# The order of VectorE, ScalarE and GpSimd in a decoder layer, taken from the scheduler with its simulated timeline switched on

## The chip, the cores and the metric

The kernel runs on one core of one Trainium2 chip. A core has five engines that each work through a queue of their own: TensorE (PE in the profile: matmuls and transposes; its loads of stationary operands are shown as PEld), VectorE (DVE), ScalarE (ACT), GpSimd (POOL) and SyncE (SP, which here only issues transfers). The metric is the device time of one execution in microseconds, as the median of several runs. Besides, one execution of each kernel is profiled; its time and its span (from the first to the last instruction) are given with it.

## The reference

It is one decoder layer in float32, with a batch of 32 sequences of 100 tokens, 256 wide:

```python
x = x + attn(layernorm(x))                    # 16 heads of 16, rotary positions, causal
x = x + xattn(layernorm(x), ctx, ctx)         # 16 heads, 361 context rows a sequence
x = x + soft_moe(layernorm(x))                # 8 experts of 128 slots each, 1024 hidden
```

The first attention has four projections (Wq, Wk, Wv, Wo) and a rotation of the queries and keys. The second has the same projections with biases, and its keys and values come from `ctx`. The third step is a soft mixture of experts: the normalised tokens are scored against 8 x 128 slot embeddings, a softmax over the tokens forms each slot, every slot goes through its expert's two layers with an exact GELU between them, and a softmax over the slots brings the results back to the tokens.

## The kernel before

**Tiles and stages.** The sequences are worked on in eight groups of four. For each group and each of the eight experts, `run_expert` multiplies the slots of four sequences (512 columns) by the first weight matrix in eight chunks (`ph`, line 893), applies GELU on ScalarE (`hT`, line 899), and multiplies by the second (`pe`, line 910). `route` (line 839) prepares an expert's slots (`dT`, `cT`, `disp`, `slT`), and `combine` (line 920) adds its result to the tokens (`py`, `x`).

**Six streams.** While the experts of one group run, the attention work of the next is fitted between the matmuls. It is written as Python generators: `self_attention` (line 487), `cross_softmax` (678), `crossing` (756), `cross_queries` (656), `cross_context` (669) and `prepare` (773, logits for the routing). Each yields a time before which its next step is not wanted. The function `between` inside the main loop (line 983) is called after every matmul of an expert and advances the streams whose time has come, by a count of TensorE time that the kernel keeps itself (`pe["t"]`). This fixes the order in which instructions are recorded.

**What fixes the order in the queues.** The kernel is built with the Tile layer. It takes the recorded instructions, works out who depends on whom, gives out the buffers of each pool in turn and places the semaphores. Every matmul and transpose is recorded through these two helpers, which pin it behind whatever was recorded on TensorE before it:

```python
def matmul(out, lhsT, rhs, share=1, **kw):                                    # line 87
    tc.keep_in_program_order(nc.tensor.matmul(out, lhsT=lhsT, rhs=rhs, **kw))
def transpose(out, in_, identity):                                            # line 91
    tc.keep_in_program_order(nc.tensor.transpose(out, in_, identity))
```

Instructions of the other engines are not pinned. Where several of them could go next on an engine, Tile's scheduler chooses when the program is built, and it may choose another order than the recorded one. On the chip, nothing is chosen any more.

**The steps that the change and the prediction touch.** In the first attention, `layer_norm` (line 315) makes `xh` on VectorE and GpSimd: statistics (306, 308), then `ve`, `rstd` and `xh` on GpSimd (310, 312, 318). TensorE transposes it, ScalarE copies `xhT` out of the bank (330), TensorE projects `ps_qk`, VectorE and GpSimd rotate (`ropeu`, `ropet`: 392 to 395), and ScalarE writes the rotated keys:

```python
nc.scalar.activation(                                                         # line 398
    kT[:, :, r, :], by(t)[:, 1], AF.Copy, scale=half[:, r : r + 1]            # rotk, read by the next sc
)
```

After the score matmuls `sc` come the mask (430), a maximum (436), a subtraction on GpSimd (437), the exponential on ScalarE (441), a sum (442) and its inverse `wide` (344). `self_turn` transposes the probabilities in four parts (`ps_pT`), and ScalarE copies each (`pT`, line 460). In the second attention, `context` transposes the context (`ps_cT`; copied as `ctxT`, 552) and projects the keys (`ps_kT`; copied with a bias as `kT`, 564); scores `xsc` are reduced (`xnmax`, 612) and exponentiated (`xp`, 617), turned (`xpT`, 633 and 635) and multiplied. `tokens` (742) makes the normalised tokens `xn` for the experts on GpSimd (310, 312, then 747 to 752), which TensorE transposes again.

At the start, `load_constants` (205) issues the loads of all attention weights and of the slot embeddings `se` from ScalarE's queue, `slots` (259) squares these on ScalarE (264) and scales them on VectorE (269) before TensorE turns them (`ps_sn`). SyncE issues the loads of `x` (292), of the context (534, 538) and of the experts' weights and biases (721 to 725). Each load counts on one of eight semaphores in turn, and a load waits at its issue until the one before it on the same semaphore has landed.

TensorE results go to banks of PSUM, 128 x 512 each: four for the scores, and two pools of two (`mm` and `big`) that `bank` (95) hands out. A bank is written again only after the copy out of it is done. ScalarE needs one table of functions for the exponential and another for GELU, so a change between them shows as an ACT_TABLE_LOAD.

## Time and profile before

| what | value |
|---|---|
| median of 3 runs | 3285.83 us (3285.1 to 3289.5) |
| profiled execution, its own time | 3288.43 us |
| its span | 3286.7 us |
| TensorE matmuls busy | 3087.9 us, 94% |
| VectorE, ScalarE, GpSimd busy | 1271.9, 1464.3, 547.1 us |
| mean granted TensorE clock | 0.979 |
| costliest groups: `pe` (L88), `ph` (L88) | 1047.6 us in 4096 matmuls, 1003.8 us in 2048 |
| ACT_TABLE_LOAD at the GELU line (L899) | 147, mean 1283 ns |

The page names an instruction by its line, its engine, and its output and inputs, with buffer numbers left out. The list of waits gives, for each engine, which result it was idle for: the total in us, how often, and the longest one. The order of time gives start, duration, engine, line and operation of merged instructions, and in brackets the idle time of the engine before them with the work that ended it. A float32 matmul shows as two passes, a transpose as one.

### The profile page before, as it was taken

To read this page: it belongs to the slowest core of one execution; us is meant where nothing else is said; L and a number is where in the kernel's file an instruction comes from. 1 tells how busy PE (TensorE), PEld (TensorE's weight loads), DVE (VectorE), ACT (ScalarE), POOL (GpSimd) and SP (SyncE) were. 2 spreads that over 40 slices of the span, in tenths; PEclk is the share of its full clock that TensorE was granted. 3 is DMA by queue.
4 is the path that set the end of the run, shared out by engine and by line. 5 is a ranking of instruction groups with operands and counts; after the bars stand their busy time and mean duration, and the time that the engine had idled before them with its cause. 6 is when DMAs were issued, how large, how long until landed. Compare 5 with 4: busy or idle time off the path is not lost.

```text
span 3286.7 us, 45298 instructions
## 1 busy us (share of the span) xinstructions
PE 3087.9 (94%) x18737; PEld 2158.8 (66%) x18737; DVE 1271.9 (39%) x2477; ACT 1464.3 (45%) x2846; POOL 547.1 (17%) x720
## 2 busy tenths in 40 slices
PE   5779999999999999999899999999899999999999
PEld 4656666665667666776666766667666766667666
DVE  3554443343433344334343344433443433332211
ACT  2444444444544544444454544544354444434331
POOL 3321321032111221012110121102311111100000
PEclk9789999999999999999999999999999999999999
DMA  3001111111111211212111111112111121112121
GB/s 107 5 10 32 45 43 57 48 42 47 55 50 42 69 45 42 64 43 67 43 45 51 61 49 47 55 50 63 41 54 47 45 64 55 42 59 68 61 64 57
DMA packets 116318, 167.55 MB, mean 51 GB/s; under 512 B 4520, under 2 KB 99728, under 8 KB 116112
## 3 DMA queue, kind: packets, MB, share of 16 engines
q1 hardware_dynamic: 112368, 161.01, 15.4%
q10 hardware_dynamic: 3744, 3.65, 0.4%
q8 instruction: 147, 2.41, 0.3%
q14 instruction: 59, 0.48, 0.0%
HBM read 161.36 MB, written 3.28 MB: 50 GB/s over the span
## 4 chain that ended last, share of the span: by engine, by line
PE 78%; ACT 10%; DVE 5%; POOL 4%; issue 2%; DMA 0%; ACTq 0%; DVEq 0%; POOLq 0%
PE pe L88 24%; PE ph L88 22%; PE sl L88 3%; PE ps_xpT L92 3%; PE py L88 3%; ACT xp L617 3%; PE xsc L88 3%; PE ps_xv L88 2%; PE ps_xav L88 2%; ACT L899 2%; PE ps_lt L88 2%; DVE xnmax L612 2%; PE ps_o L88 2%; PE ps_qk L88 2%; ACT hT L899 2%
## 5 line engine op out<-in xcount | busy, mean ns | idle before, releaser
L88 PE MATMUL pe<-w,hT 128*128 128x256 f32 x4096 | 1047.6, 388 | 15.3 <-ACT hT L899 14.9
L88 PE MATMUL ph<-slT,w 128*128 128x512 f32 x2048 | 1003.8, 604 | 29.1 <-ACT hT L899 28.8
L88 PEld LDWEIGHTS pe<-w,hT 128*128 128x128 f32 x4096 | 738.8, 192 | 169.6 <-issue 62.9
L899 ACT ACTIVATE hT<-ph,cols 128x512 f32<-128x512 f32 x512 | 350.0, 688 | 531.0 <-PE ph L88 508.6
L88 PEld LDWEIGHTS ph<-slT,w 128*128 128x128 f32 x2048 | 356.9, 191 | 294.3 <-issue 213.4
L617 ACT ACTIVATE xp<-xsc,xnmax 100x361 f32<-100x361 f32 x512 | 280.9, 563 | 116.5 <-DVE xnmax L612 80.6
L612 DVE TENSOR_REDUCE xnmax<-xsc 100x2 f32<-100x722 f32 x256 | 220.8, 899 | 166.2 <-PE xsc L88 165.4
L92 PEld LDWEIGHTS ps_xpT<-ident,xp 100*128 100x128 f32 (+1 forms) x1536 | 175.6, 153 | 114.2 <-issue 75.5
L635 DVE COPY xpT<-ps_xpT 128x400 f32<-128x400 f32 (+1 forms) x256 | 144.0, 570 | 211.3 <-PE ps_xpT L92 210.6
L899 ACT ACT_TABLE_LOAD x147 | 188.6, 1283 | 78.5 <-PE ph L88 76.2
L916 DVE TENSOR_TENSOR eo<-pe,b 128x512 f32<-128x512 f32 x128 | 87.9, 687 | 338.7 <-PE pe L88 338.3
L92 PE MATMUL ps_xpT<-ident,xp 100*128 100x100 f32 (+1 forms) x1536 | 192.0, 254 | 9.2 <-ACT xpT L633 5.8
L929 DVE SCALAR_TENSOR_TENSOR x<-py,cinv,x 100x256 f32<-100x256 f32 x256 | 112.2, 479 | 193.1 <-PE py L88 193.1
L856 POOL TENSOR_TENSOR dT<-dT,ri 128x400 f32<-128x400 f32 x64 | 54.4, 852 | 765.2 <-DVE ri L855 666.0
L437 POOL TENSOR_TENSOR p<-p,nmax 100x800 f32<-100x800 f32 x64 | 96.1, 1522 | 384.1 <-DVE nmax L436 382.2
L310 POOL TENSOR_SCALAR ve<-bnmv 100x1 f32<-100x1 f32 x96 | 21.4, 225 | 799.4 <-DVE bnmv L308 797.6
L88 PEld LDWEIGHTS sl<-disp,xn 100*128 100x128 f32 x1024 | 134.5, 194 | 14.9 <-DVE x L929 4.2
L849 POOL TENSOR_TENSOR cT<-lt,nmB 128x400 f32<-128x400 f32 x64 | 66.0, 1038 | 466.1 <-PE py L88 319.2
L88 PE MATMUL sl<-disp,xn 100*128 100x128 f32 x1024 | 137.4, 278 | 4.5 <-DVE x L929 2.7
L88 PE MATMUL xsc<-kT,xqT 32*100 32x361 f32 x1024 | 112.7, 510 | 22.8 <-ACT xp L617 21.0
L88 PE MATMUL py<-eo,cT 128*100 128x256 f32 x512 | 132.4, 381 | 1.0 <-DVE eo L916 0.8
L874 DVE TENSOR_SCALAR slT<-sl,cols 128x512 f32<-128x512 f32 x128 | 95.8, 749 | 72.5 <-PE sl L88 72.3
(140 smaller groups left out, 3457.4 us busy)
## 6 DMA issues: line engine op xcount, KB each, us to landing
w<-in_L_ffn_w_dram SPq DMA_DIRECT2D x128, 1024.0 KB
ctx<-in_ctx_dram SPq DMA_DIRECT2D x32, 256.0 KB
b<-in_L_ffn_b_dram SPq DMA_DIRECT2D x64, 128.0 KB
ctx<-in_ctx_dram SPq DMA_DIRECT2D x32, 105.0 KB
x<-in_x_dram SPq DMA_DIRECT2D x8, 400.0 KB
out_dram<-x SPq DMA_DIRECT2D x16, 200.0 KB
se<-n_L_ffn_slot_embeds_dram ACTq DMA_DIRECT2D x1, 1024.0 KB
rawWk<-in_L_attn_Wk_dram ACTq DMA_DIRECT2D x1, 256.0 KB
```

Of the source, the lines that this page charges most:

```text
L88: tc.keep_in_program_order(nc.tensor.matmul(out, lhsT=lhsT, rhs=rhs, **kw))
L92: tc.keep_in_program_order(nc.tensor.transpose(out, in_, identity))
L437: nc.gpsimd.tensor_tensor(p[:, hs, :], p[:, hs, :], nmax[:, hs].unsqueeze(2).to_broadcast([S, HPC, S]), ALU.subtract,)
L612: nc.vector.tensor_reduce(nmax[:, c, q : q + 2, r], sc[:S, q : q + 2, :SK], axis=AX.X, op=ALU.max, negate=True,)
L617: nc.scalar.activation(p[:, q, :], sc[:S, q, :SK], AF.Exp, bias=nmax[:, c, q, r : r + 1], accum_out=sums[:, c, q, r : r + 1],)
L635: nc.vector.tensor_copy(pT[:n], ps[:n, : HG * S])
L849: nc.gpsimd.tensor_tensor(cT, k.lt[e], k.nmB, ALU.add)
L856: nc.gpsimd.tensor_tensor(dT, dT, ri.unsqueeze(2).to_broadcast([P, nb, S]), ALU.mult)
L874: nc.vector.tensor_scalar(slT[:, dc, :], sl[:, : nb * NS], cols[:, NGM + dc : NGM + dc + 1], None, ALU.mult)
L899: nc.scalar.activation(h[:, :n], ph_[:, :n], AF.Gelu, bias=cols[:, e * NHC + hc : e * NHC + hc + 1])
L916: nc.vector.tensor_tensor(eo[:, :m], po[:, :m], b2.unsqueeze(1).to_broadcast([P, m, D]), ALU.add)
L929: nc.vector.scalar_tensor_tensor(xg[g][:, b, :], py[:S, i, :], k.ci[:, b : b + 1], xg[g][:, b, :], ALU.mult, ALU.add,)
```

## The change

The scheduler of the Tile layer is told to run a simulated timeline while it puts the instructions in order. Which instruction of an engine counts as ready, when the scheduler looks for the next one, then comes from that timeline. The instructions, their tiles and the order in which they are recorded stay as they are.

```diff
-    with _tile.TileContext(nc) as tc:
+    with _tile.TileContext(nc, schedule_with_timeline_sim=True) as tc:
         decoder_layer(tc, aps, *outs)
```

In the built program TensorE's instructions stand in the same order as before. Those of VectorE, ScalarE and GpSimd stand in a partly different one, four transfers of SyncE change places near the start, and table loads fall where ScalarE's new order needs them. The semaphores follow from the order.

## The prediction

> **What bounds the kernel now.** I read the busy table, then the waits of TensorE alone, then the order of time around the longest of them.
>
> ```profile
> span 3286.7 us, 45298 instructions
> ...
> PE 3087.9 (94%) x18737; PEld 2158.8 (66%) x18737; DVE 1271.9 (39%) x2477; ACT 1464.3 (45%) x2846; POOL 547.1 (17%) x720
> ```
>
> TensorE is the bound: 94% of the span, the others 45% at most. All that another order of VectorE, ScalarE and GpSimd can win is the remaining 199 us of TensorE idle time, 78 of it before 280 us (the windows of 20 us sum to 202.4 busy of 280), some 20 of those before any input is there. The rest is about 3 to 5 us in each 100. In the waits of TensorE (total us, times, longest) the top lines are these.
>
> ```profile
> PE ps_qk L88 <- ACT xhT L330: 34.0, 5, 22.9
> PE ph L88 <- ACT hT L899: 28.8, 28, 1.7
> PE ps_pT L92 <- ACT kT L564: 22.0, 4, 7.2
> PE xsc L88 <- ACT xp L617: 21.0, 17, 3.0
> PE pe L88 <- ACT hT L899: 14.9, 12, 2.2
> ```
>
> The third matters most: four waits, 22.0 us, so three of them are 7.2 us long. The order of time finds them at 779.07, 1568.99 and 2360.56 us, once every two groups. The first, on TensorE, then on ScalarE, then on GpSimd:
>
> ```profile
> 771.25 0.62 PE L88 MATMUL pe<-w,hT 128*128 128x256 f32 x2
> 779.07 0.91 PE L92 MATMUL ps_pT<-ident,p 100*100 100x100 f32 x4 [7.20 <-ACT kT L564]
> ```
> ```profile
> 777.75 0.81 ACT L398 ACTIVATE rotk<-ropet,half 128x200 f32<-128x200 f32 x2 [10.38 <-POOL ropet L395]
> 778.47 0.54 ACT L564 ACTIVATE kT<-ps_kT,cols 128x361 f32<-128x361 f32 x1
> 778.92 0.48 ACT L460 COPY pT<-ps_pT 100x400 f32<-100x400 f32 x1
> ```
> ```profile
> 774.39 1.24 POOL L318 TENSOR_SCALAR xh<-x,bnmv,rstd 100x256 f32<-100x256 f32 x1
> 775.59 1.02 POOL L394 TENSOR_TENSOR ropeu<-ropeu,rope 128x400 f32<-128x400 f32 x1
> 776.70 1.02 POOL L395 TENSOR_TENSOR ropet<-ropet,ropeu 128x400 f32<-128x400 f32 x1
> ```
>
> The matmuls of ps_kT had ended by 770.6. The copy out of their bank (kT, L564) stood behind rotk (L398), which waited 10.38 us for GpSimd, which worked off a string of layer-norm steps first. TensorE needed the bank.
>
> [...] The trace has 1283 ns as the mean of a load[...] (the load at 1216.06 us is followed by a GELU at 1217.35), so I charge 1.28 us. [...] I therefore take TensorE from starts: at 783.66 to 784.12 us the same pair of pe passes took 0.46 us from start to next start, so of 779.07 - 771.25 = 7.82 us some 7.4 is lost, against 7.20 shown; I use 7.2.
>
> **The change, part by part.** No operation is added or removed but table loads. From the built programs: all 10921 matmuls stand in the same order (each is pinned); of the other instructions 511 of 2445 on VectorE, 301 of 2014 on ScalarE (table loads apart), 305 of 720 on GpSimd and 4 of some 280 transfers on SyncE change place, by at most 11. So the question is where the first TensorE reader of each moved result stands. I went through the three queues and SyncE's in the new order: each instruction keeps its own duration from the trace, starts when the one ahead is through and its inputs are there, and hands on with the delays that the trace shows (34 to 95 ns); matmuls keep their start-to-start distances. The same treatment of the old order finds the old waits; I use differences alone.
>
> Rotk and kT. The new order at 779 us (and alike at the other two) is kT, four pT copies (L460), then rotk. kT then starts when ps_kT is done, the bank is free at about 771.3, and 7.2 us of idle go, three times: -21.6 us. The added wait: rotk stands behind the third and fourth pT copies, which wait for TensorE, so it comes about 1.7 us after its input. Behind it waits a copy of xnT (L330) that is not due yet. Its reader is the matmul group sc at 814.10 us, over 30 us on: it costs nothing.
>
> GELU before exponentials. At 1218 us TensorE waits for hT:
>
> ```profile
> 1215.17 0.87 ACT L441 ACTIVATE p<-p 100x800 f32<-100x800 f32 x1 [0.61 <-POOL p L437]
> 1216.06 1.28 ACT L899 ACT_TABLE_LOAD   x1
> 1217.35 1.27 ACT L899 ACTIVATE hT<-ph,cols 128x512 f32<-128x512 f32 x2
> ```
>
> The new order puts that first hT ahead of both exponentials of p. Waits of 0.9 (445 us), 2.2 (1218) and 2.2 (2010) go: -5.3 us. In all there are 302 table loads instead of 294; 8 x 1.28 = 10.3 us on an engine that is 45% busy. Were ScalarE late at every one of them, +10.3 would be the upper end; most replace idle time, and where they make a copy late it is in the rest below.
>
> The start. Now eight squares (L264) that wait for slot embeddings until 30.68 us keep the xhT copy back to 33.89, and TensorE waits 22.9 us. In the new order xhT comes before them. But ScalarE issues the embeddings' load later: its issue waits for the transfer of x (L292) that landed at about 26 us and that now has another place among the load semaphores, so the copies of ctxT and xhT end at about 28.9 and TensorE goes on 5.3 us earlier. The embeddings land 10.5 us after their issue (20.15 to 30.66 before), about 36.8; the squares (8 x 0.39), their scaling (L269, 8 x 0.27) and so ps_sn come 3.6 us late. With the later small gains and losses up to 280 us: -1.3 us. Bounds: -6 if the embeddings land as early as before, +5 if x lands 5 us later. Moving the ctx loads ahead of x on SyncE by two places is in this; nobody needs that ctx before 49 us.
>
> Late xn. GpSimd now takes the layer-norm chains of several sequences step by step side by side, with xn (L752) last. At 663 us two xh (1.23 each), an addition (0.81) and one ve and rstd (0.23 + 0.56) go ahead of it: 4.1 us, and its reader waited 0.33 us already, so none is covered. 22 of 32 xn come 0.8 to 7.7 us later, but most have room: +4.2 at 663, +1.2 at 2747, +0.4 at 1451 and 2243, together +6.2 us.
>
> The rest, some fifty places of both signs (+3.4 at 398 and +2.6 at 450 for xhT behind four exponentials; -2.8 at 349 and -2.7 at 549 for copies set free; +0.9 twice where wide, L344, is later and a wait of 4.6 us grows), adds to -3.8 us by the same working. It hangs on single tenths, so I count half: -2.
>
> Sum: -21.6 - 5.3 - 1.3 + 6.2 - 2 = **-24 us**. The profiled execution took 3288.4 us, 1.7 more than its span, and gives 3264.4; the median of the runs is 2.6 lower, so I predict **3262 us**. An early stall taken from TensorE stays won, as its later order is fixed[...].
>
> **Rivals.** *Given back.* The three waits go, but the start costs +5 and the rest is +5 instead of -2: -21.6 - 5.3 + 5 + 6.2 + 5 = -11, 3275 us. For it: most late copies sit in the first 700 us, where TensorE's idle share is largest; against: that stretch nets -1.1 by my working. *The wait moves.* If the pT copy rather than kT gates TensorE, or GpSimd is late to another reader at the same places, only the small gains stay: -2 to -6, 3282 us. Against: the pT copy now before 779 had its input at 771.4, and takes 0.48 us. A change without effect is excluded by the number of moved instructions. *Slower: GpSimd's chains.* Place: xn at the 32 ends of a sequence. Six are already late (9 us if TensorE were not shifted, 6.2 as counted); the next have room of 1.1, 3.6, 3.6 and five times 4.8 us. Were each xn d us later than its durations say, the cost is 6d + (d-1.1) + 2(d-3.6) + 5(d-4.8): at d = 4.8 it is 35 us, over the 24 won by more than 6.6. So it decides from about 4.8 us on, more than a third of a burst of 9 to 13 us; GpSimd's steps are steady in the trace. It gives 3294 us or more.
>
> **How the numbers follow.** Forecast 0.73, given back 0.15, wait moves 0.07, slower 0.05. 0.2% (6.6 us) is about what a measurement of this kernel can tell from no change. The first two are faster by more than that, so faster 0.88, within 0.07, slower 0.05. Handing on with doubled delays in both orders turns the sum to -31, and the early landing adds -5, so the low end is -38, 3248; the high end is the given-back case with a little more, 3277.
>
> **What would show it.** Right: no 7.2 us wait of ps_pT on kT; pe on hT with nothing above 1.5; ps_qk's longest about 17 to 18 us; ps_sn waiting for se some 3.6 us near 40 us; ps_xhT on POOL xn with a wait of about 4 near 660; 302 table loads; TensorE's busy time as before, and its idle time near 175. Wrong: the pT transposes at about 772, 1555 and 2340 us waiting on another engine for several us, or xn waits in every group.

## The result and the profile after

The changed kernel took 3266.09 us (median of 4 runs, 3265.5 to 3266.6) against 3285.47 us before (4 runs, 3283.9 to 3289.5): a ratio of 0.9939, 95% interval 0.9922 to 0.9956, 19.4 us less. The forecast was 3262 us, 24 us less than the median before. The total is near; several of the terms behind it, as the runs below show, are not.

The page of the changed kernel, the span and the busy table:

```profile
span 3264.1 us, 45284 instructions
...
PE 3079.0 (94%) x18737; PEld 2154.7 (66%) x18737; DVE 1273.4 (39%) x2477; ACT 1478.3 (45%) x2854; POOL 544.1 (17%) x720
```

TensorE's matmuls are the same 18737 passes (the 4096 and 2048 in the table before count passes as well), and yet their busy time fell by 8.9 us (3087.9 before). Its idle time fell by 13.7 us, from 198.8 to 185.1. I had forecast some 24 us of idle time and nothing in the busy time. ScalarE has eight instructions more, the eight table loads. All 302 take 1283 ns, and 301 of them stand where a GELU follows an exponential or an exponential a GELU (293 of 294 before); the other is ScalarE's first, at L552.

TensorE's waits in the changed kernel (result waited for, total us, times, longest):

```profile
PE ps_qk L88 <- ACT xhT L330: 32.7, 10, 13.7
PE ph L88 <- ACT hT L899: 26.5, 25, 1.7
PE xsc L88 <- ACT xp L617: 21.4, 20, 3.0
PE ps_xhT L92 <- POOL xn L752: 16.2, 9, 4.4
PE ps_rb L92 <- DVE wide L344: 13.0, 3, 5.8
PE pe L88 <- ACT hT L899: 8.1, 9, 1.1
```

The wait of ps_pT for kT (22.0 us) is gone, and pe waits 8.1 us for hT instead of 14.9. Two other lines grew: ps_xhT waits 16.2 us for xn (0.7 before), ps_rb 13.0 us for wide (9.1 before). ps_qk still waits 32.7 us for xhT (34.0 before), but in ten waits where there were five: the long one at the start fell from 22.9 to 13.7 us, and others came.

The place of the first long wait in the changed kernel, on TensorE, then on ScalarE (four copies pT, L460, stand between the two lines of ScalarE):

```profile
771.53 0.62 PE L88 MATMUL pe<-w,hT 128*128 128x256 f32 x2
771.99 0.51 PE L92 MATMUL ps_pT<-ident,p 100*100 100x100 f32 x4
```

```profile
770.95 0.56 ACT L564 ACTIVATE kT<-ps_kT,cols 128x361 f32<-128x361 f32 x1 [3.30 <-PE ps_kT L88]
...
777.06 0.81 ACT L398 ACTIVATE rotk<-ropet,half 128x200 f32<-128x200 f32 x2 [1.08 <-POOL ropet L395]
```

kT is copied as soon as ps_kT is done (at 770.95 us, 778.47 before), and ps_pT follows pe without a wait.

### The profile page after: what moved, and what is told of

The parts are those of the page before. It is cut to its first block, busy times and chain, and to the rows that moved or that the text cites. A ratio compares the mean times of both kernels' runs of the same rounds, so it can differ in the third digit from the quotient of the medians.

```text
span 3264.1 us, 45284 instructions
## 1 busy us (share of the span) xinstructions
PE 3079.0 (94%) x18737; PEld 2154.7 (66%) x18737; DVE 1273.4 (39%) x2477; ACT 1478.3 (45%) x2854; POOL 544.1 (17%) x720
## 4 chain that ended last, share of the span: by engine, by line
PE 76%; ACT 12%; DVE 5%; POOL 3%; issue 2%; DMA 2%; ACTq 0%; DVEq 0%; POOLq 0%; SPq 0%
PE pe L88 23%; PE ph L88 23%; PE sl L88 3%; PE ps_xpT L92 3%; ACT xp L617 3%; PE py L88 3%; PE xsc L88 3%; ACT L899 2%; PE ps_xv L88 2%; PE ps_lt L88 2%; PE ps_xav L88 2%; PE ps_kT L88 2%; ACT hT L899 2%; PE ps_o L88 2%; PE ps_qk L88 2%
## 5 line engine op out<-in xcount | busy, mean ns | idle before, releaser
L88 PE MATMUL pe<-w,hT 128*128 128x256 f32 x4096 | 1036.2, 385 | 8.4 <-ACT hT L899 8.1
L88 PE MATMUL ph<-slT,w 128*128 128x512 f32 x2048 | 1003.2, 604 | 27.6 <-ACT hT L899 26.5
L88 PEld LDWEIGHTS pe<-w,hT 128*128 128x128 f32 x4096 | 731.4, 190 | 158.1 <-issue 64.1
L899 ACT ACT_TABLE_LOAD x151 | 193.7, 1283 | 77.1 <-PE ph L88 74.6
L929 DVE SCALAR_TENSOR_TENSOR x<-py,cinv,x 100x256 f32<-100x256 f32 x256 | 111.9, 478 | 178.9 <-PE py L88 178.5
L88 PEld LDWEIGHTS sl<-disp,xn 100*128 100x128 f32 x1024 | 133.8, 194 | 16.3 <-DVE x L929 5.1
L633 ACT COPY xpT<-ps_xpT 128x400 f32<-128x400 f32 x128 | 62.6, 489 | 164.4 <-PE ps_xpT L92 164.2
```

What stands on the lines that cost most here:

```text
L633: nc.scalar.copy(pT[:n], ps[:n, : HG * S])
L899: nc.scalar.activation(h[:, :n], ph_[:, :n], AF.Gelu, bias=cols[:, e * NHC + hc : e * NHC + hc + 1])
L929: nc.vector.scalar_tensor_tensor(xg[g][:, b, :], py[:S, i, :], k.ci[:, b : b + 1], xg[g][:, b, :], ALU.mult, ALU.add,)
```

## Where busy time can fall: the clock behind a wait

One observation is needed for all that follows. These are stretches of the kernel before around its first 7.2 us wait (stretch, its length, TensorE's busy time and matmul passes, granted clock, DMA share, GB/s):

```profile
768.00:772.00 4.00, 3.87 (x23) 1.00 0.12 47
772.00:776.00 4.00, 0.00 (x0) 1.00 0.00 0
776.00:780.00 4.00, 0.93 (x5) 0.57 0.00 0
780.00:784.00 4.00, 4.00 (x14) 0.57 0.00 0
784.00:788.00 4.00, 4.00 (x26) 1.00 0.00 0
```

TensorE stops at 771.9. For the next 4 us the granted clock is 1.00, then it falls to half, and it stays there for most of 780 to 784 us, when work goes on again: 14 passes in 4 us where the next stretch has 26. Eight passes of pe take 3.67 us from 779.76, and 1.92 us from 784.46. So the matmuls behind this wait of 7.2 us are slower as well; where e11 below fills the wait, the clock stays at 1.00. Behind 300 us, the traces of the kernel before and of the changed one have 20 waits of TensorE of 2 us or more. All ten of 3.44 to 7.20 us come with half clock, which begins 2.3 to 5.4 us after TensorE stops and ends 2.9 to 6.6 us after it goes on. Of the three of 2.96 to 3.16 us, two have a half clock that begins 2.4 and 3.8 us after the stop, and of the seven of 2.18 to 2.76 us, two have one that begins 3.7 and 3.9 us after it. What decides between these was not shown. In the kernel before, the clock stays at 1.00 behind the 2.2 us wait at 1216 us, while another 2.2 us wait, which ends at 1669 us, has 3.4 us of half clock behind it. Stretches behind the one and the other (columns as above):

```profile
1218.00:1222.00 4.00, 3.91 (x24) 1.00 0.53 217
1671.00:1674.00 3.00, 3.00 (x13) 0.50 0.04 8
1674.00:1677.00 3.00, 3.00 (x19) 0.95 0.00 0
```

I added up the stretches at half clock over each whole trace, and TensorE's busy time in them; half of that busy time is counted as lost, which is an estimate from such pairs as the eight passes of pe above (3.67 us and 1.92). The clock's records begin at 16 to 43 us, depending on the kernel, and nothing is counted ahead of them. Differences are against the kernel before, for the one profiled execution of each kernel.

| kernel | span, us | idle time, difference | busy time, difference | lost at half clock before 300 us / behind |
|---|---|---|---|---|
| before | 3286.7 | 0 | 0 | 36.8 / 19.7 |
| changed | 3264.1 | -13.7 | -8.9 | 33.1 / 13.4 |
| e1, rotk moved alone | 3254.4 | -21.7 | -10.6 | 32.7 / 14.7 |
| e5, GpSimd's order put back | 3252.6 | -14.4 | -19.7 | 21.1 / 14.6 |
| e6, xhT ahead of exponentials | 3248.3 | -23.5 | -14.9 | 33.1 / 9.1 |
| e8, searched orders | 3180.7 | -77.0 | -29.0 | 32.7 / 6.5 |

In the changed kernel 56.5 - 46.5 = 10.0 us less is lost at half clock, against 8.9 us less busy time. So the clock accounts for it. Not all of it is the change's: before 300 us, four traces with the old order there (before, e1, e4, e11) lose 30.7 to 36.8 us, and six with the changed order there (changed, e2, e3, e6, e9, e13) 29.3 to 36.0. In e8 the clock accounts for 17.3 of the 29.0 us; where the rest comes from was not traced.

## The experiments

My theory after the result: the three freed banks carry the gain, and late copies elsewhere give part of it back. The first rival was that a free bank only moves the wait to the next copy or to rotk's own readers; a second, formed on the traces, that part of each gain is the clock's.

In all kernels an order is held by edges between neighbours of one queue, without waits. The scheduler has no choice left, and each kernel differs from its base in orders alone, unless its edit says more:

```diff
+    for a, b in zip(seq, seq[1:]):
+        tc.add_manual_dep(b, a.name, edge, reason="impose")
```

The diffs below show the queue, not the code. Each run was compared with the kernel before on its own chip (medians 3285.2 to 3286.7 us).

**e1: the three places alone.** Before's orders, and at 778, 1568 and 2360 us:

```diff
 ScalarE
-rotk, rotk (L398)
 kT (L564)
 pT, pT, pT, pT (L460)
+rotk, rotk (L398)
```

> The order of the kernel before on VectorE, ScalarE, GpSimd and SyncE, held by ordering edges, with one change: at the three places near 779, 1569 and 2360 us ScalarE takes kT (L564) and the four pT copies (L460) before rotk (L398), as in the kernel after. Theory (the freed bank): this alone gives most of what the whole change gave; three waits of 7.2 us go, at each place up to 1.3 us comes back behind it, so 17 to 21.6 us less than the kernel before, 3264 to 3268 us. Rival (spread out): the wait is only moved on, since TensorE finds the next late result, and the 19 us of the change come from many small places; then this gives less than 8 us, 3278 us or more.

Measured: 3259.11 us (5 runs, 3256.1 to 3262.7), ratio 0.9919 (0.9905 to 0.9932). Three moved places win more than the whole change, and more than the 17 to 21.6 us of the theory. I compared the start of every TensorE instruction in the two traces; a step is a change of the lead that one kernel has over the other. There are three steps of 7.36 us, none of 0.8 us or more elsewhere behind 40 us, and no loss at the next ps_xhT, where the changed kernel loses 1.35 us each time. These steps make 22.1 us; the rest of the 27.6 us against its own runs before is about what is less lost at half clock behind 300 us (5.0 us in the trace). Another 4.1 us less are lost before 300 us, where no order differs; they are chance. It is the bank of kT that TensorE waited for and not the pT copy, though e1 moves both: in the kernel before ps_pT starts at 779.07, 0.06 us behind the end of kT, while the pT copy runs until 779.40.

**e2: the change without the three places.** The changed kernel's orders, rotk ahead of kT again there.

> The orders of the kernel after, held by ordering edges, with ScalarE's old order (rotk ahead of kT and pT) put back at the three places only. Theory: 17 to 21.6 us more than the kernel after, 3283 to 3288 us, so the whole change without these three is worth 2 us or less. Rival (spread out): less than 8 us more, 3274 us or less.

Measured: 3291.36 us (21 runs, 3286.2 to 3296.5), ratio 1.0015 (1.0009 to 1.0022). The wait is back:

```profile
PE ps_pT L92 <- ACT kT L564: 18.5, 3, 6.2
```

All of the rest of the change, some 250 places in the four queues, is together a loss of 4.7 us. The three places are worth 25.3 us within the changed kernel (24.1 if each of the two kernels is taken against the runs of before on its own chip).

**e3 and e4: by stage.** e3 has the changed orders up to 290 us and the old ones behind it, e4 the reverse.

> The orders of the kernel after up to 290 us on all queues, those of the kernel before from there on. In the trace of the kernel after TensorE is 9 to 12 us ahead between 40 and 160 us and 4.0 us ahead at 280. Theory: only the last counts, so 4 us less than the kernel before, 3281.5 us. Rival: part of the early lead was lost to later changes and is kept with the old order, 8 us or more less, 3277 us or less.

> The old order up to 290 us, the changed kernel's from there on (the complement of the run with the changed start alone, which was 5.75 us faster than before). Theory (stages add, since the queues run empty at the stage's end): 19.4 less 5.75, so 13.6 us faster than before, near 3272. Rival (the start's order decides how late the streams stand against each other later, so the parts do not add): beyond 3267 to 3277.

Measured: e3 3280.91 us (18 runs), ratio 0.9981 (0.9974 to 0.9988), 5.8 us less; e4 3269.66 us (5 runs), ratio 0.9955 (0.9942 to 0.9967), 15.5 us less. Together 21.2 against the 19.4 of the whole change: within 2 us the stages add, and e3 is nearer to its theory (4 us) than to its rival (8 us or more). The start is worth 5.8 us alone, 3.6 as the difference of e4 to the changed kernel, and 1.3 were forecast.

**e5 and e13: GpSimd's order.** e5 puts 27 of 33 places of GpSimd's queue back to the old order (the other six, at 39 to 91 and at 240 us, stay as changed; the expectation counts 29); e13 only the 25 of them behind 290 us. At 661 us, in both:

```diff
 GpSimd
-ve, ve, rstd, rstd, rstd, q, xh, xh, q, x, r, r, xn
+rstd, q, q, r, ve, r, rstd, xn, xh, ve, rstd, xh, x
```

> The orders of the kernel after, but GpSimd's old order back at 29 of the 33 places where the two differ (all with xn; the four left are at 39 to 91 us). The prediction charged 6.2 us to late xn. Theory (late xn costs what was charged, less what another wait takes over): 4 to 6 us less than the kernel after, 3260 to 3262 us. Rival (covered): another late result stands at the same place, no change, 3266 us.

> The changed kernel's orders, with GpSimd's old order at the 25 places behind 290 us alone (the earlier run with GpSimd's order put back had also the two places near 157 and 187 us, and gained 10 us, nearly all of it before 300 us by its trace). Theory (the late xn chains behind 300 us cost nothing of lasting effect: where xn comes in time, TensorE stands as long a few us later, for x at sl): within 2 us of the changed kernel, 3264 to 3267. Rival (the prediction's fourth step: late xn costs 6.2 us at 663, 1451, 2243 and 2747 us): 3260 or less.

Measured: e5 3256.08 us (4 runs, 3254.3 to 3258.5), ratio 0.9906 (0.9892 to 0.9919), 10.0 us less than the changed kernel, where the theory had 4 to 6; e13 3266.38 us (5 runs, 3262.6 to 3269.3), ratio 0.9943 (0.9929 to 0.9956), the changed kernel's time. So late xn behind 290 us costs nothing that lasts. First the changed kernel, then e13 in TensorE's order of time, at the place with the longest wait:

```profile
665.14 0.59 PE L92 MATMUL ps_xhT<-ident,xn 100*128 100x100 f32 x2 [4.41 <-POOL xn L752]
666.15 3.03 PE L88 MATMUL ps_lt<-xnT,snT 128*128 128x200 f32 x8 [0.41 <-ACT xnT L330]
```

```profile
661.11 0.39 PE L92 MATMUL ps_xhT<-ident,xn 100*128 100x100 f32 x2 [0.98 <-POOL xn L752]
663.94 2.34 PE L88 MATMUL ps_lt<-xnT,snT 128*128 128x200 f32 x8 [2.43 <-ACT xnT L330]
```

With xn in time ps_xhT waits 3.4 us less, and the next product waits 2.0 us more for the copy of its result. Elsewhere it is x (L929): sl waits 6.5 us for it in e13, 2.3 in the changed kernel. e5 and e13 differ at two places alone, at 157 and 187 us of the kernel before, and by 10.3 us. There ps_xhT comes 1.9 and 1.5 us earlier in e5, since xn is in time, but most of the difference is busy time: e5's idle time is only 0.7 us below the changed kernel's. The changed kernel, then e5 (columns as above):

```profile
100.00:150.00 50.00, 38.32 (x357) 0.83 0.03 8
150.00:200.00 50.00, 40.18 (x406) 0.83 0.03 9
```

```profile
100.00:150.00 50.00, 39.59 (x453) 0.93 0.03 9
150.00:200.00 50.00, 40.22 (x390) 0.97 0.04 11
```

The clock is higher in e5. But one of the changed kernel's stretches of half clock, at 124 us, lies ahead of the first of the two places, where the orders are alike. So how much of the 10.3 us the two places bring, and how much comes of when the half clock falls, stays open. Two things speak for the places: e5 loses 21.1 us at half clock before 300 us, where the six traces with the changed order there lose 29.3 to 36.0; and all four runs of e5 have mean clocks of 0.983 to 0.986, all four of the changed kernel 0.981 or 0.982.

**e6: xhT ahead of exponentials.** The changed kernel with the old order at six places of ScalarE's queue, of which this one, near 390 us, is the dearest:

```diff
 ScalarE
-hT (L899), p (L441)
+p (L441), hT (L899)
-xp, xp, xp, xp (L617), xhT (L330)
+xhT (L330), xp, xp, xp, xp (L617)
```

> The changed kernel's orders, with ScalarE's old order at six places: the xhT copies near 396 us ahead of the four cross-attention exponentials again, the exponentials ahead of GELU near 393 and 444 us, and ahead of kT and GELU at 822, 1611 and 2403 us. Theory (the trace's steps of 5.3 us at 398, 2.7 at 450 and 1.0 at 826, 1615 and 2407 are losses of the change that the forecast undersized): 8 us faster than the changed kernel, near 3258. Rival (those late copies are waited for only because the engine came early, and something else ends at the same time): within 2 us of the changed kernel, near 3265.

Measured: 3249.76 us (4 runs, 3247.5 to 3250.1), ratio 0.9889 (0.9875 to 0.9902): 16.3 us less than the changed kernel, twice the theory's figure. ScalarE in the changed kernel, then TensorE:

```profile
383.41 1.28 ACT L441 ACT_TABLE_LOAD   x1
384.71 0.87 ACT L441 ACTIVATE p<-p 100x800 f32<-100x800 f32 x1
385.60 1.28 ACT L899 ACT_TABLE_LOAD   x1
386.89 0.69 ACT L899 ACTIVATE hT<-ph,cols 128x512 f32<-128x512 f32 x1
387.60 1.28 ACT L617 ACT_TABLE_LOAD   x1
...
391.05 0.34 ACT L330 COPY xhT<-ps_xhT 128x200 f32<-128x200 f32 x1
```

```profile
391.44 2.03 PE L88 MATMUL ps_qk<-xhT,wTWq 128*128 128x100 f32 x8 [5.57 <-ACT xhT L330]
393.26 1.91 PE L88 MATMUL ps_qk<-xhT,wTWk 128*128 128x100 f32 x8
```

And the same on TensorE in e6:

```profile
386.64 1.03 PE L88 MATMUL ps_qk<-xhT,wTWq 128*128 128x100 f32 x8
387.51 1.06 PE L88 MATMUL ps_qk<-xhT,wTWk 128*128 128x100 f32 x8
```

GELU and the exponentials alternate in the changed kernel, so two more table loads stand in front of the copy, and then four exponentials with a load of their own. TensorE waits 5.57 us, and then the same eight passes take 2.03 us instead of 1.03: the half clock again. By the two traces e6 is 4.8 us ahead where ps_qk begins, and 7.4 at the product of 397 us, where the changed kernel is at full clock again. Over the whole trace e6 has 9.8 us less idle and 6.0 us less busy time than the changed kernel.

**e9: the GELU first.** The changed kernel with the old order where a GELU had been put ahead of exponentials of p, at 444 (one p), 1217 and 2009 us:

```diff
 ScalarE
-hT (L899), p, p (L441)
+p, p (L441), hT (L899)
```

> The changed kernel's orders, with ScalarE's old order at the three places where the change put a GELU (hT, L899) ahead of exponentials (near 445, 1217 and 2009 us). Theory (the prediction's second step: each GELU moved forward shortens the one wait for its hT and the gain lasts): 5.3 us slower than the changed kernel, near 3271. Rival (the exponentials put back behind the GELU make the next product on them late, so the gain is handed back within the round): within 1 us of the changed kernel, near 3266 to 3267; the trace then shows the step of 2 us at the GELU and a step the other way a few us later.

Measured: 3267.54 us (5 runs, 3263.2 to 3268.7), ratio 0.9942 (0.9930 to 0.9955), 1.5 us above the changed kernel, which these runs do not tell from nothing. The rival holds in the main. The changed kernel, then e9, at the third place:

```profile
1993.15 0.59 PE L88 MATMUL pe<-w,hT 128*128 128x256 f32 x2
1996.60 1.14 PE L88 MATMUL ps_qk<-xhT,wTWq 128*128 128x100 f32 x8 [0.50 <-ACT xhT L330]
2000.19 0.87 PE L88 MATMUL xsc<-kT,xqT 32*100 32x361 f32 x8 [0.68 <-ACT xp L617]
```

```profile
1996.45 0.70 PE L88 MATMUL pe<-w,hT 128*128 128x256 f32 x2 [2.19 <-ACT hT L899]
1999.34 1.03 PE L88 MATMUL ps_qk<-xhT,wTWq 128*128 128x100 f32 x8
2002.09 0.87 PE L88 MATMUL xsc<-kT,xqT 32*100 32x361 f32 x8
```

e9 is 3.30 us behind at pe, but only 2.74 at ps_qk and 1.90 at xsc. The steps at pe are 1.09, 2.36 and 2.36 us at the three places. At the second and the third, 0.66 us come back at ps_qk and 0.75 at xsc within seven us, so 0.95 of each 2.36 is kept; at the first, 0.88 and 2.58 us come back at ps_xhT and ps_qk, more than was won. A copy put forward had put another one back. The clock adds to this: in e9 the wait of 2.19 us at the second place has 3.4 us of half clock with it, the equal one at the third has none.

**e11: the wait filled.** The kernel before, its order unchanged, with 15 more matmuls in each of the three long waits, so that TensorE does not stand (each of the three sums of pe takes one product in 16 times):

```diff
+        if calls["n"] in (2753, 5475, 8197):
+            for _ in range(15):
+                nc.tensor.matmul(out, lhsT=lhsT, rhs=rhs, start=False, stop=False)
         nc.tensor.matmul(out, lhsT=lhsT, rhs=rhs, **kw)
```

> The kernel before, its orders held, with the three 7.2 us waits left where they are and filled: ahead of the second expert product (pe) that stands in front of each, 15 more copies of that same product are added to its sum, 45 matmuls in all, 0.43 us each (so those three sums of pe count one product 16 times). Theory ([...]in the kernel before the records show 0.5 from 777 to 783, 1565 to 1572 and 2357 to 2364 us, with 4.3, 2.9 and 3.2 us of matmuls in them): the half clock does not come, and the kernel with 45 more matmuls is 5 us faster than before, 3280. Rival (the granted clock in the records does not lengthen the matmuls behind a wait): as before, 3285 to 3286, or slower by what the copies overshoot.

Measured: 3278.75 us (11 runs), ratio 0.9978 (0.9969 to 0.9986). With 45 more matmuls the kernel is 6.4 us faster, near the theory's 5. Its order of time at the first place (line numbers are shifted by the added code; the two lines of pe, 16 matmuls of two passes, fill the wait; ps_pT waits 0.74 us; the granted clock is 1.00 from 768 to 788 us):

```profile
766.19 6.66 PE L93 MATMUL pe<-w,hT 128*128 128x256 f32 x30
772.70 0.59 PE L96 MATMUL pe<-w,hT 128*128 128x256 f32 x2
774.03 0.55 PE L101 MATMUL ps_pT<-ident,p 100*100 100x100 f32 x4 [0.74 <-ACT kT L573]
```

Behind 300 us, 13.0 us instead of 19.7 are lost at half clock. So the wait of 7.2 us itself and the slower matmuls behind it are two costs, and the second is about 2 us for each of the three (6.7 us less lost, or 6.4 us less time, by three).

**e7 and e8: better orders.** e7 takes the old order at 39 of the 251 places where the kernels differ, the new one elsewhere. e8 adds 68 stretches, 53 of them on ScalarE, in an order that neither kernel has.

> The changed kernel's orders at most places and the old order at 39 of the 251 places where the two differ: 6 on GpSimd (the xn chains among them), 16 on ScalarE (the six places of the copies ahead of exponentials among them) and 17 on VectorE, chosen by walking the four queues with the durations of the profile. The three freed banks stay. Theory (what the change loses comes from late xn, late xhT copies and a few late VectorE steps, and each loss can be taken back alone): 28 us faster than the changed kernel, near 3238. Rival (the losses are not additive, or are the clock's): no faster than with GpSimd's old order alone, 3256.

> As the kernel with the old order at 39 places, and at 68 more stretches (ScalarE 50 or so, VectorE and GpSimd the rest) an order that neither kernel has, found by moving one instruction at a time in a walk of the four queues where TensorE waits longest. Theory (the time is set by the order in which ready work stands in the four queues, with the durations as they are): 57 us faster than the changed kernel, near 3209. Rival (the walk lacks waits that only the chip has, or the waits removed come back elsewhere): between 3230 and 3260.

Measured: e7 3219.48 us (5 runs, 3217.9 to 3219.9), ratio 0.9798 (0.9784 to 0.9811); e8 3181.27 us (4 runs, 3173.2 to 3185.4), ratio 0.9679 (0.9665 to 0.9693). Both fell by more than expected. e8's waits of TensorE:

```profile
PE xsc L88 <- ACT xp L617: 22.2, 18, 3.0
PE ps_qk L88 <- ACT xhT L330: 17.7, 5, 13.3
...
PE pe L88 <- ACT hT L899: 4.4, 7, 0.9
PE ph L88 <- ACT hT L899: 3.1, 10, 0.6
```

The 25 waits of ph for hT, 26.5 us in the changed kernel and never above 1.7 us each, are nearly gone.

**e12: the start kept at work.** e8 with small products of the identity in front of 19 instructions that wait for an operand, 113 in all:

```diff
+        for _ in range(FILL.get(calls["n"], 0)):
+            nc.tensor.matmul(out[:, :c], lhsT=ident[:, :m], rhs=ident[:, :c], start=True, stop=True)
```

> The orders of the kernel with the searched orders (3181), and ahead of 19 TensorE instructions that wait for an operand, 16 of them in the first 250 us, 113 small products of the identity with itself (128x100), 1 to 32 at a place and sized to 80% of the wait at half clock, written where the waiting product then writes. They take part in no result. Theory (in the first 300 us TensorE works 65 us at half clock, since it stands too often; keeping it at work raises the granted clock there): 5 to 20 us faster than the searched orders alone, 3161 to 3176. Rival (the first stage is bound by the other engines' chains, and a faster TensorE only waits longer): within 3 us of 3181.

Measured: 3167.36 us (5 runs, 3164.9 to 3171.1), ratio 0.9640 (0.9627 to 0.9653), 13.9 us less than e8. e8, then e12:

```profile
0.00:100.00 100.00, 61.06 (x411) 0.85 0.29 88
100.00:200.00 100.00, 85.54 (x867) 0.88 0.03 9
200.00:300.00 100.00, 83.72 (x590) 0.90 0.06 19
```

```profile
0.00:100.00 100.00, 76.07 (x620) 0.90 0.30 88
100.00:200.00 100.00, 86.60 (x889) 0.93 0.04 12
200.00:300.00 100.00, 86.85 (x579) 0.93 0.08 27
```

The granted clock is higher in every stretch of the start (time ahead of the first record, at 28.6 us in e8 and 16.0 in e12, counts as full clock), and 19.9 instead of 32.7 us are lost there at half clock. This kernel is the fastest of the study, 118 us below the kernel before.

## Why the prediction was right, and where it was not

| step of the prediction | forecast, us | measured, us | by |
|---|---|---|---|
| rotk and kT, three waits | -21.6 | -27.6 alone, -25.3 within the change | e1, e2 |
| GELU before exponentials | -5.3 | -1.5, not told from 0 | e9 |
| the start | -1.3 | -5.8, or -3.6 | e3, e4 |
| late xn | +6.2 | 0 (25 places behind 290 us); up to +10.3 from two places before | e13, e5 |
| the rest | -2 | +16.3 in six of its places | e6 |
| sum | -24 | -19.4 (the whole change) | |

The measured steps, with e1's figure, 0 for late xn and e3's start, add to -18.6 (e6 and e9 share the place at 444 us; what the two xn places bring is within the start). That the sum came near is luck in part: a loss that I had not sized is in the main made up by gains that I had sized too small and by the charge for late xn, which did not fall due. The other places of the rest were never run alone. By e2 everything but the three places is +4.7 us; less -1.5, -5.8 and +16.3, some -4 us is left for them, so that the rest is about +12 us, an estimate from differences of medians, where I had -2.

*Rotk and kT.* Right in mechanism and place: 7.36 us at each of 779, 1569 and 2361 us, and rotk's own reader does not wait. The term was too small because I priced the wait alone. The clock behind it, about 2 us each by e11, was not in the sum. So the 199 us of idle time were not all that an order can win: it won busy time as well.

*GELU.* The waits of pe for hT fell as forecast. But I took the saving as kept, since "an early stall taken from TensorE stays won". It doesn't where the instruction moved back on the same queue is the next one due: by e9's trace, 1.41 of each 2.36 us are lost again within seven us, and at 445 us more than had been won. Here the sentence failed.

*The start.* Too small. I had x land at about 26 us and xhT with it at about 28.9. In the trace of the changed kernel ScalarE issues the embeddings' load, which waits for x, at 22.39 us, and its xhT copy starts at 24.81. ps_qk then waits at most 13.7 us, not 17 to 18, and ps_sn 2.2 us for se, not 3.6.

*Late xn.* GpSimd's steps are steady (64 xh of 1218 to 1251 ns before, 1216 to 1343 in the changed kernel). The wait came as said (4.41 us near 665), and more of it than counted: 16.2 us in nine waits. I took every one as a loss; e13 shows that with xn in time TensorE waits for xnT or x instead. A wait in the list is not a gain to be had. At 157 and 187 us it may have been a loss: there e5 makes xn early again, and it is 10.3 us faster than e13, a part of which I cannot assign. My term had neither place by name.

*The rest.* The step that failed most. I had the places (+3.4 at 398, +2.6 at 450 for xhT behind exponentials), but undersized them, and set them against gains of equal size elsewhere. The waits of ps_qk there were 5.6 and 3.4 us, and each came with half clock (0.50 from 390 to 397 and from 448 to 455 us). The profile puts the second down to xrinv of VectorE; with ScalarE's old order there, in e9, it is 0.87 us and for xhT. Two of the eight added table loads, for which the sum has no term of their own, stand ahead of the first. The expectations failed alike: 8 us for e6, where 16.3 were measured, since I still read the price of a wait as its length.

Of the signs named in the prediction, those of kT, of pe, of xn and of 302 table loads came; those of ps_qk and ps_sn did not. "TensorE's busy time as before, and its idle time near 175" did not either: busy 8.9 us lower, idle 185.1. Of the rivals, "the wait moves" is excluded by e1 and e2, the slower one through GpSimd by the result itself, since it says 3294 us or more. "Given back" describes what happened, from another place: not the start as a whole but the copies of xhT. One sum of mine is off: -31 and -5 make -36 and a low end of 3250, not -38 and 3248.

## What to carry to other kernels

A ready copy out of a PSUM bank behind an instruction that waits for another engine is worth looking for first: three such places, with waits of 7.2 us, made all of the gain of 250 moves, and moving them alone was faster than the new scheduler order. Price a long wait of TensorE at its length plus the slower matmuls behind it (here about 2 us behind each wait of 7.2 us; behind 300 us, all ten waits of 3.44 us or more in the traces before and after the change had half clock with them, and four of the ten of 2.18 to 3.16 us). Test a suspected wait by taking it away before it counts as a gain, since the next input can be late as well (in e13, 3.4 us less for xn and 2.0 us more for xnT). Where TensorE must stand often, as at the start, small products that nobody needs can pay for themselves: 113 of them took 13.9 us off e8.

## What the runs showed of the hardware that I had not expected

- The half clock comes 3.3 to 4.7 us after TensorE stops in the three long waits of the kernel before, and it outlasts the wait by 2.9 to 4.3 us. In the changed kernel eight passes of ps_qk took 2.03 us behind a 5.57 us wait, and in e6 1.03 us without it.
- Behind a wait of 2.2 us it may stand or not: of six such waits in the kernel before, those that end at 1669 and 2461 us have 3.4 us of half clock behind them, the other four none.
- More work was less time: 45 more matmuls in three waits made the kernel 6.4 us faster, 113 small ones made e8 13.9 us faster.
- Runs of one kernel differ along with the granted clock: the 21 runs of e2 go from 3286.2 us at a mean clock of 0.980 to 3296.5 us at 0.977. Four traces with the same order up to 290 us (before, e1, e4, e11) lose 30.7 to 36.8 us at half clock before 300 us.
